# Convolution after attention, one core: q's first block by three queues, band 8 of the second convolution by the two-row way, paired outer products copied by one instruction

## The chip, the cores and the metric

The kernel runs on one core of a Trainium2 chip. The metric is the device time of one execution in microseconds, given as the median of several runs. A profile of one execution lies beside it. The page calls TensorE PE (its weight loads PEld), VectorE DVE, ScalarE ACT, GpSimd POOL and SyncE SP.

## What is computed

The input has 4 images of 128 channels and 64 x 64 pixels, all fp32. Layer 0 is attention, layer 1 a residual block of two 3 x 3 convolutions:

```python
# layer 0
x_norm = _group_norm(x, norm_w, norm_b)                      # 8 groups
qkv = jnp.einsum('oc,bchw->bohw', qkv_w, x_norm) + qkv_b     # 4 heads of 32
attn = jax.nn.softmax(jnp.einsum('bhid,bhjd->bhij', q, k) * scale, axis=-1)
out = jnp.einsum('oc,bchw->bohw', proj_w, attn_times_v) + proj_b
x = x + out
# layer 1
out = conv3x3(x, lsq_quantize(w1, alpha1))                   # 9 taps, pad 1
out = relu(batchnorm(out, gamma1, beta1))                    # mean and variance over all images
out = conv3x3(out, lsq_quantize(w2, alpha2))
out = relu(batchnorm(out, gamma2, beta2) + x)
```

Both batch norms need the mean and the variance over all images before anything after them can start, so each convolution ends in a short serial step.

## The kernel before, in words

**Attention** takes some 2200 us. It goes over 32 blocks (4 images of 8 blocks of 512 query pixels), and in each over 32 steps of 128 key pixels, with two pairs of heads in a step. `scores` (lines 435 to 449) makes the products of one pair (the tiles `s`) and ACT takes their exponential; `weights` (line 461) multiplies by v. `run_scores(3)` and `run_weights(3)` alternate to the end. The order is written out by hand (`manual_schedule`): every engine does its instructions in program order, and waits come from the tiles that they share.

**The first block** is special, because nothing can be hidden ahead of it. `project_parts` makes k, q and v of a chunk of 512 pixels on PE; `parts` (lines 353 to 361) takes a product out of PSUM twice: ACT writes its rounded part and DVE what is left (`kst`, `qst`). For chunk 0 `direct` (lines 396 to 409) then spreads these by eight transfers over the partitions of the tile that the score products read. Their issue alternates between SP and POOL. For q each transfer is 128 KB, and they are written in the order group 0 (four of them), group 1 (four). The first score pair reads group 0 and the second group 1. The later chunks of k go by way of DRAM (`kd`, line 361, stored by SP at this stage, and loaded by `load_k`, line 416). All this is emitted in the order k of chunk 0, q of chunk 0, k 1, v 0, k 2, v 1, k 3, v 2, k 4, v 3.

**A convolution** goes over 16 bands of 16 rows (4 images of 4 bands). fp32 rows are split into a rounded part (hi) and a remainder (lo), and PE does both. There are two ways:

- A *plain* band has 2 tiles of 18 matmuls each, 36 in all. Preparing it (`split_parts`) is one ACT copy for hi (line 619) and one DVE subtraction for lo (line 622). Its statistics are taken by two `bn_stats` on DVE (line 955), and ACT copies the two tiles to `cv` (line 961).
- A *mixed* band makes two output rows at a time out of four products over mixed input rows, with 24 matmuls (`conv_by_two`, line 870). `mixed_parts` prepares it: DVE makes `vo` and the two halves of `vi` (lines 600 to 603), ACT copies both as hi (`uo`, `ui`, line 605), and DVE subtracts for lo and li (line 609). `rows_of_two` (lines 874 to 904) puts the rows together. `copy`: ACT copies the second inner product into the odd rows of `cv`. `inner`: DVE makes even and odd rows from it and the first inner product, with their sums (lines 887 and 889). `outer`: ACT copies the two outer products to `co` with their sums (line 894), and a POOL transfer adds `co` to `cv` in place (line 896). For bands 13 and 14 `outer_at_once` does that addition on DVE instead (line 900). Later ACT squares the band for the variance (line 1011); that is kept in a list (`behind`) and done about two bands later by `flush(1)`, because it must wait for the transfer.

`BY_TWO` (line 584) says which bands are mixed: 2 to 14 in the first convolution, 2 to 14 without 8 in the second. (Band 1 of the first has plain products and its sums from ACT, lines 964 and 968.) `banks` (line 978) gives a band its PSUM: the inner products take two adjoining banks from the pool `pss` (3 tiles of two banks). The outer products take, in turns, another `pss` tile (names ending in z) or two single banks from `psa` (x and y).

`layer` (lines 932 to 1049) is the loop over bands. In band m it emits PE's matmuls of band m, then `copy`, in the first convolution a `flush(1)`, then `begin` (the mixing for band m + 2 with ACT's hi copies), `flush(1)`, `inner`, `rest` (lo and li of band m + 2), `later` (in the first convolution the load of band m + 3, in the second ACT's normalisation of band m + 3, line 1138), and `outer`. After band 14 come the squares that are left, sums on DVE (lines 1027 to 1035), band 15 as two tiles `c_last` with `bn_stats` on DVE (line 1041), and `batch_norm`. Band 15 is prepared in band 13 (`split_parts`).

After the second convolution `load_res` (line 1175) has brought the residual back, and the output goes out chunk by chunk (lines 1201 to 1203).

Of the kernel before, what the change touches and what calls it, by code (L numbers as in the profile page):

```python
# [16 lines left out]
F32 = mybir.dt.float32  # L17
AF = mybir.ActivationFunctionType
ALU = mybir.AluOpType
# [3 lines left out]
P = 128  # L23
# [4 lines left out]
FB = 512  # L28
# [50 lines left out]
def _fast_body(ctx, tc, x, norm_w, norm_b, qkv_wt, qkv_b, proj_wt, proj_b,  # L79
               w1, alpha1, gamma1, beta1, w2, alpha2, gamma2, beta2, out, cnt):  # L80
    nc = tc.nc
    B, C, H, W = x.shape
# [131 lines left out]
    pss = ctx.enter_context(tc.tile_pool(name="pss", bufs=3, space=PSUM))  # L214
# [11 lines left out]
    sums = att.enter_context(tc.tile_pool(name="sums", bufs=2))  # L226
# [5 lines left out]
    def f32(t):  # L232
        return t.bitcast(F32)
# [154 lines left out]
    def k_tile(b, j):  # L388
        ks[b, j] = stack_tile(f"k{b}_{j}")[:, : 2 * FB].rearrange("p (g n) -> p g n", n=FB)
        return ks[b, j]  # L390
# [5 lines left out]
    def direct(what, t):  # L396

        u = k_tile(0, 0) if what == "k" else q_tile(0, 0)
        engines = nc.sync, nc.gpsimd
        for g in range(2):  # L400
            for c, s in enumerate((0, 2, 1, 3)):
                i, part = divmod(s, 2)
                h = 2 * g + i
                src = t[h * D : (h + 1) * D, :, :]
                eng = engines[(4 * g + c) % len(engines)]
                if what == "k":
                    eng.dma_start(out=f32(u)[s * D : (s + 1) * D, g, :], in_=src[:, part, :])
                else:
                    eng.dma_start(out=f32(u)[s * D : (s + 1) * D, g, :, :], in_=src)
# [152 lines left out]
    def raw_band(i, b, g):  # L562
        mixed = b * (H // BR) + g in BY_TWO[i]
        t = stack_tile(f"t{i}_{b}_{g}")
# [13 lines left out]
    raw, ready = {}, {}  # L578
# [2 lines left out]

    BY_TWO = set(range(2, 15)), set(range(2, 15)) - {8}

    def mixed_parts(t, name):

# [45 lines left out]
    def parts_of(i, m, t):  # L633
        b, g = bandlist[m]
        way = mixed_parts if m in BY_TWO[i] else split_parts
        mix, rest, ready[i, b, g] = way(t, f"{i}_{b}_{g}")
        return mix, rest
# [225 lines left out]
    def conv_by_two(parts, a, c, i):  # L863

        for m, ps, w in ((1, a[0], wmix[:, 0, :, :]), (2, a[1], wmix[:, 1, :, :]),
                         (0, c[0], wq[i][:, 0:3, :]), (3, c[1], wmix[:, 2, :, :])):
            n = 0
            for part in parts:
                for kw in range(3):
                    nc.tensor.matmul(ps.rearrange("p (r w) -> p r w", w=W), w[:, kw, :],  # L870
                                     part[m][:, :, kw : kw + W], start=(n == 0), stop=(n == 5))
                    n += 1

    def rows_of_two(a, c, y, sums, name, at_once):

        def of(t, e):
            return t.rearrange("p (r e w) -> p r e w", e=2, w=W)[:, :, e, :]

        even, odd = of(y, 0), of(y, 1)
        a0, a1, c0, c1 = (u.rearrange("p (r w) -> p r w", w=W) for u in (*a, *c))  # L880
        outer_rows = f32(stack_tile(f"co{name}"))[:, : 2 * FB]

        def copy():
            nc.scalar.copy(odd, a1)

        def inner():
            nc.vector.scalar_tensor_tensor(even, odd, 1.0, a0, ALU.mult, ALU.add,
                                           accum_out=sums[:, 0:1])
            nc.vector.scalar_tensor_tensor(odd, odd, -1.0, a0, ALU.mult, ALU.add,
                                           accum_out=sums[:, 1:2])  # L890

        def outer():
            for e, u in enumerate((c0, c1)):
                nc.scalar.activation(of(outer_rows, e), u, AF.Identity,
                                     accum_out=sums[:, 2 + e : 3 + e])
            nc.gpsimd.dma_start(out=y, in_=outer_rows, accum_op=ALU.add)

        def outer_at_once():
            for e, u, v in ((0, even, c0), (1, odd, c1)):
                nc.vector.scalar_tensor_tensor(u, u, 1.0, v, ALU.mult, ALU.add,  # L900
                                               accum_out=sums[:, e : e + 1])

        return copy, inner, outer_at_once if at_once else outer, outer_rows
# [26 lines left out]
    def layer(i, prepare, start=None):  # L930


        on_act = {1} if i == 0 else set()
        plain = [m for m in range(len(bandlist) - 1) if m not in BY_TWO[i] and m not in on_act]
        two = [m for m in range(len(bandlist) - 1) if m in BY_TWO[i] or m in on_act]
        st = mid.tile([P, 2 * len(plain), 6], F32, name=f"st{i}")
        sums = mid.tile([P, 4 * len(two)], F32, name=f"sums{i}")
# [39 lines left out]
        def banks(m):  # L977
            b, g = bandlist[m]
            a = conv_tile(i, b, g)
            if (len(two) - 1 - two.index(m)) % 2:  # L980
                c = [psa.tile([P, FB], F32, name=f"c{i}_{b}_{g}{j}", tag="a") for j in "xy"]
            else:
                c = pss.tile([P, 2, FB], F32, name=f"c{i}_{b}_{g}z", tag="s")
                c = [c[:, j, :] for j in range(2)]
            return [a[:, j, :] for j in range(2)], c

        done = start(banks, stats, keep, origin) if start else {}
        for m, (b, g) in enumerate(bandlist[:-1]):
            if m in done and m not in BY_TWO[i]:
                continue  # L990
            begin, rest, later = prepare(m)
            if m in BY_TWO[i]:
                if m in done:
                    a, c = done[m]
                else:
                    a, c = banks(m)
                    conv_by_two(ready[i, b, g], a, c, i)
                y = cv[b][:, 2 * g * FB : (2 * g + 2) * FB]
                k = two.index(m)
                copy, inner, outer, junk = rows_of_two(a, c, y, sums[:, 4 * k : 4 * k + 4], f"{i}_{m}",  # L1000
                                                       m > 12)
                copy()
                if i == 0:
                    flush(1)
                begin()
                flush(1)
                inner()
                rest()
                later()
                outer()  # L1010
                behind.append(lambda y=y, k=k, junk=junk: nc.scalar.activation(  # L1011
                    junk, y, AF.Square, bias=shift[:, 1:2], accum_out=squares[:, k : k + 1]))
                continue
            ps = conv_tile(i, b, g)
            for j in range(2):
                conv(ready[i, b, g], ps[:, j, :], j, wq[i])
            begin()
            flush(1)
            rest()
            later()  # L1020
            for j in range(2):
                stats(m, j, ps)
                keep(m, j, ps)
            if m == 0:
                origin()
# [10 lines left out]
        b, g = bandlist[-1]  # L1036
        for j in range(2):
            ps = psa.tile([P, FB], F32, name=f"c{i}_last{j}", tag="a")
            conv(ready[i, b, g], ps, j, wq[i])
            c = 2 * g + j  # L1040
# [53 lines left out]
    def opening(banks, stats, keep, origin):  # L1094
        last = parts[len(blocks) - 1]
        last["merge"]()
        e = [conv_tile(0, *bandlist[m]) for m in range(2)]
        conv(ready[0, 0, 0], e[0][:, 0, :], 0, wq[0])
        begin, rest = parts_of(0, 2, raw[bandlist[2]])
        begin()  # L1100
        load_band(*bandlist[3])
        conv(ready[0, 0, 0], e[0][:, 1, :], 1, wq[0])
        mix_weights(0)
        rest()
        last["residual"]()
        for j in range(2):
            stats(0, j, e[0])
            keep(0, j, e[0])
        origin()
        conv(ready[0, 0, 1], e[1][:, 0, :], 0, wq[0])  # L1110
        last["sums"](0)
        last["sums"](1)
        last["spread"]()
        begin, rest = parts_of(0, 3, raw[bandlist[3]])
        begin()
        load_band(*bandlist[4])
        conv(ready[0, 0, 1], e[1][:, 1, :], 1, wq[0])
        rest()
        last["invert"]()
        last["gather"]()  # L1120
        for j in range(2):
            stats(1, j, e[1])
            keep(1, j, e[1])
        done = banks(2)
        conv_by_two(ready[0, 0, 2], *done, 0)
        begin, rest = parts_of(0, 4, raw[bandlist[4]])
        begin()
        rest()
        load_band(*bandlist[5])
        return {0: None, 1: None, 2: done}  # L1130

    a1, c1 = layer(0, first, opening)
# [14 lines left out]
    for r0, r1 in ((0, RB + 2), (RB + 2, BR + 2)):  # L1147
        a, e = max(r0 + g0 * BR - 1, lo_row), min(r1 + g0 * BR - 1, hi_row)
# [45 lines left out]
    for b in range(B):  # L1194
        for j in range(4):
            ends = (b, j) in ((0, 0), (B - 1, 3))
            for p in range(2 if ends else 1):
                n = HN // 2 if ends else HN
                y = res[b, j][:, p * n : (p + 1) * n]
# [463 lines left out]
```

## Time and profile before

| what | us |
|---|---|
| median of 3 runs (2469.05 to 2471.85) | 2470.35 |
| the profiled execution itself | 2469.57 |
| its span, first to last instruction | 2467.9 |
| attention, to PE's last `acc` product | 2226.7 |
| first convolution, to PE's last `c_last` product | 2226.7 to 2330.4 |
| second convolution, to PE's last `c_last` product | 2334.0 to 2437.3 |
| last statistics and output | 2437.3 to 2467.9 |

| engine | busy us | share of the span |
|---|---|---|
| PE | 2432.5 | 99% |
| DVE | 2197.6 | 89% |
| ACT | 2182.4 | 88% |
| POOL | 300.3 | 12% |

The time outside the span (2469.57 less 2467.9) is 1.7 us. The ends of matmuls are modelled and consecutive matmuls overlap, so the spacing of PE's starts is used for what PE needs, and not the mean duration of one matmul. In a row of the timeline the first number is the start in us from the span's beginning, the second the duration; what stands in brackets is the idle time of the engine before it, and what ended it.

### The profile page before, as it was taken

The numbers are of one execution on the slowest core, as the hardware profiler recorded it, in microseconds if no ns is written. First come the engines' busy times: TensorE is split into PE (matmuls) and PEld (weight loads), VectorE is DVE, ScalarE is ACT, GpSimd is POOL, SyncE is SP. The second block draws the span as 40 slices with busy tenths as digits, with TensorE's granted clock in tenths as the row PEclk, the third lists the DMA queues.
The fourth block names the chain that finished last, engine by engine and source line by source line (L and its number), as shares of the span: only waits on it lengthen the run. The fifth ranks groups of instructions, "written<-read, shape, count | busy, mean of one in ns | idle before, by whom it ended". The sixth has DMA issues, their size and how long they took to land.

```text
span 2467.9 us, 65119 instructions
## 1 busy us (share of the span) xinstructions
PE 2432.5 (99%) x28396; PEld 1445.7 (59%) x28396; DVE 2197.6 (89%) x1560; ACT 2182.4 (88%) x2446; POOL 300.3 (12%) x527
## 2 busy tenths in 40 slices
PE   9999999999999999999999999999999999999995
PEld 6555555555555555555555555555555555557774
DVE  6899888989998888899989888898999999999897
ACT  5999888999988899999998899999999999996686
POOL 1111111111101111111101111111010100111110
PEclk9999999999999999999999999999999999999997
DMA  6887677678776766688767676678666666766627
GB/s 195 191 191 167 172 176 176 167 187 210 169 164 167 181 161 163 145 205 205 172 151 175 173 175 156 156 190 204 149 141 147 149 138 144 160 150 167 162 56 236
DMA packets 128389, 416.21 MB, mean 169 GB/s; under 512 B 33808, under 2 KB 34960, under 8 KB 99424
## 3 DMA queue, kind: packets, MB, share of 16 engines
q0 software_dynamic: 48688, 292.38, 52.3%
q1 hardware_dynamic: 78832, 118.54, 17.1%
q8 instruction: 225, 3.69, 0.6%
q10 hardware_dynamic: 576, 1.05, 0.1%
q14 instruction: 68, 0.56, 0.1%
HBM read 107.75 MB, written 56.43 MB: 67 GB/s over the span
## 4 chain that ended last, share of the span: by engine, by line
PE 93%; DVE 3%; DMA 2%; issue 1%; ACT 0%; SPq 0%; POOL 0%; POOLq 0%; ACTq 0%; DVEq 0%
PE s L447 43%; PE acc L461 39%; PE c L837 2%; PE c L870 1%; DMA rm<-p 1%; PE pk L322 1%; PE l L493 1%; PE pq L322 1%; PE pv L322 1%; PE po L322 1%; PE c_last L837 1%; DVE res L1201 1%; DVE li L609 0%; DVE lo L609 0%; DMA cv<-co 0%
## 5 line engine op out<-in xcount | busy, mean ns | idle before, releaser
L449 ACT ACTIVATE p<-s 128x1024 f32<-128x1024 f32 x2048 | 1951.3, 1033 | 197.3 <-PE s L447 153.1
L476 DVE TENSOR_TENSOR r<-r,p 128x2048 f32<-128x2048 f32 x768 | 1757.9, 2289 | 63.1 <-ACT p L449 12.0
L447 PE MATMUL s<-q,k 64*128 64x512 f32 x8192 | 1137.3, 409 | 1.9 <-issue 1.7
L461 PE MATMUL acc<-p,v 128*32 128x256 f32 x16384 | 1025.8, 383 | 0.0
L447 PEld LDWEIGHTS s<-q,k 64*128 64x128 f32 x8192 | 716.1, 184 | 408.3 <-issue 166.2
L461 PEld LDWEIGHTS acc<-p,v 128*32 128x32 f32 x16384 | 462.7, 109 | 483.1 <-issue 248.1
L471 POOL DMA_DIRECT2D rm<-p x160 | 140.4, 877 | 780.3 <-ACT p L449 658.2
L357 DVE SCALAR_TENSOR_TENSOR kst<-pk,b,kst 128x512 fp32r<-128x512 f32 x32 | 24.0, 751 | 80.5 <-PE s L447 61.7
L474 DVE TENSOR_TENSOR r<-p,p 128x2048 f32<-128x2048 f32 x32 | 73.2, 2287 | 8.3 <-ACT p L449 7.0
L357 DVE SCALAR_TENSOR_TENSOR qst<-pq,b,qst 128x512 fp32r<-128x512 f32 x32 | 24.0, 750 | 59.2 <-PE s L447 46.5
L361 POOL DMA_DIRECT2D qd<-qst x31 | 23.0, 742 | 267.1 <-DVE qst L357 217.7
L497 POOL DMA_DIRECT2D r<-rm x32 | 27.2, 851 | 224.6 <-PE s L447 81.2
L870 PE MATMUL c<-ui,wmix 128*128 128x512 f32 x150 | 43.9, 400 | 0.0
L870 PE MATMUL c<-li,wmix 128*128 128x512 f32 x150 | 43.8, 400 | 0.0
L361 POOL DMA_DIRECT2D kd<-kst x27 | 20.0, 741 | 177.3 <-DVE kst L357 162.1
L605 ACT CAST uo<-vo 128x1024 fp32r<-128x1024 f32 x25 | 26.3, 1054 | 16.0 <-DVE vo L600 15.0
L469 POOL DMA_DIRECT2D rm<-p x32 | 17.8, 558 | 175.2 <-ACT p L449 106.9
L1011 ACT ACTIVATE co<-cv,shift 128x1024 f32<-128x1024 f32 x25 | 28.8, 1152 | 11.1 <-DMA cv<-co 11.1
L493 PE MATMUL l<-r,ones 128*32 128x256 f32 x512 | 37.7, 379 | 0.0
L538 POOL DMA_DIRECT2D y<-x x32 | 21.0, 657 | 121.6 <-DVE x L537 112.8
L356 ACT ACTIVATE kst<-pk,b 128x512 fp32r<-128x512 f32 x32 | 22.4, 700 | 14.5 <-PE pk L322 14.5
L322 PE MATMUL po<-av,wp 128*32 128x512 f32 x256 | 33.4, 593 | 0.4 <-DVE av L527 0.4
(268 smaller groups left out, 1220.2 us busy)
## 6 DMA issues: line engine op xcount, KB each, us to landing
rm<-p POOLq DMA_DIRECT2D x192, 1024.0 KB, 7.7
r<-rm POOLq DMA_DIRECT2D x32, 1024.0 KB, 7.6
q<-qd SPq DMA_DIRECT2D x248, 128.0 KB, 4.5
x<-in_x_dram SPq DMA_DIRECT2D x86, 256.0 KB, 6.2
k<-kd SPq DMA_DIRECT2D x124, 128.0 KB, 4.8
qd<-qst POOLq DMA_DIRECT2D x31, 512.0 KB, 5.0
kd<-kst POOLq DMA_DIRECT2D x27, 512.0 KB, 4.4
cv<-co POOLq DMA_DIRECT2D x21, 512.0 KB, 4.8
```

Of the source, the lines that this page charges most:

```text
L322: nc.tensor.matmul(out[cs, :], w[:, cs], x, start=True, stop=True)
L357: nc.vector.scalar_tensor_tensor(lo, ps[what], bias, t[:, 0, :], ALU.add, ALU.subtract)
L361: (nc.sync if start else nc.gpsimd).dma_start(out=dst[b, j].rearrange("s p n -> p s n"), in_=t)
L447: nc.tensor.matmul(s[:, i, :], k[r, half, c0 : c0 + P], q[r, half, part, :], start=(part == 0), stop=(part == 1))
L449: nc.scalar.activation(pts[step][:, 2 * half : 2 * half + 2, :], s, AF.Exp, scale=SCALE)
L461: nc.tensor.matmul(acc[n][h * D : (h + 1) * D, cs], v[:, kt % KB, h * D : (h + 1) * D], pt[:, h, cs], start=(kt == 0 and half == 0), stop= ...
L471: nc.gpsimd.dma_start(out=msum[n], in_=pt, accum_op=ALU.add)
L474: nc.vector.tensor_tensor(rsum[n], pts[step - 1], pt, ALU.add)
L476: nc.vector.tensor_tensor(rsum[n], rsum[n], pt, ALU.add)
L493: nc.tensor.matmul(t["l"][h * D : (h + 1) * D, cs], ones, r[:, h, cs], start=first, stop=end)
L837: nc.tensor.matmul(ps.rearrange("p (r w) -> p r w", w=W), w[:, tap, :], part[:, r0 + kh : r0 + kh + RB, kw : kw + W], start=(n == 0), stop ...
L870: nc.tensor.matmul(ps.rearrange("p (r w) -> p r w", w=W), w[:, kw, :], part[m][:, :, kw : kw + W], start=(n == 0), stop=(n == 5))
```

## The change

Five edits:

1. `direct`: for q the four-fold cycle is SP, POOL, ACT, POOL; so SP issues two of q's eight transfers, ACT two and POOL four. k stays with SP and POOL.
2. `BY_TWO`: band 8 of the second convolution is mixed too.
3. `rows_of_two`: `copy` writes into the first half of the tile `co` instead of the odd rows of `cv`, and `inner` reads it there. `outer` overwrites that tile.
4. `outer`: where the outer products lie in one `pss` tile, one ACT instruction copies both and takes one sum.
5. `layer`: in the first convolution the `flush(1)` ahead of `begin` is left out for bands 13 and 14.

Since the second convolution then has 13 mixed bands instead of 12, and `banks` counts from the last, bands 2, 4 and 6 change places with 3, 5 and 7 as to the pool of their outer products. Bands 9 to 14 keep theirs.

```diff
-        engines = nc.sync, nc.gpsimd
+        engines = (nc.sync, nc.gpsimd) if what == "k" else (nc.sync, nc.gpsimd, nc.scalar, nc.gpsimd)
...
-    BY_TWO = set(range(2, 15)), set(range(2, 15)) - {8}
+    BY_TWO = (set(range(2, 15)),) * 2
...
-    def rows_of_two(a, c, y, sums, name, at_once):
+    def rows_of_two(a, c, both, y, sums, name, at_once):
...
+        copied = outer_rows[:, :FB].rearrange("p (r w) -> p r w", w=W)
+
         def copy():
-            nc.scalar.copy(odd, a1)
+            nc.scalar.copy(copied, a1)
 
         def inner():
-            nc.vector.scalar_tensor_tensor(even, odd, 1.0, a0, ALU.mult, ALU.add,
+            nc.vector.scalar_tensor_tensor(even, copied, 1.0, a0, ALU.mult, ALU.add,
                                            accum_out=sums[:, 0:1])
-            nc.vector.scalar_tensor_tensor(odd, odd, -1.0, a0, ALU.mult, ALU.add,
+            nc.vector.scalar_tensor_tensor(odd, copied, -1.0, a0, ALU.mult, ALU.add,
                                            accum_out=sums[:, 1:2])
 
         def outer():
-            for e, u in enumerate((c0, c1)):
-                nc.scalar.activation(of(outer_rows, e), u, AF.Identity,
-                                     accum_out=sums[:, 2 + e : 3 + e])
+            if both is not None:
+                nc.scalar.activation(
+                    outer_rows.rearrange("p (r e w) -> p e r w", e=2, w=W),
+                    both.rearrange("p e (r w) -> p e r w", w=W), AF.Identity,
+                    accum_out=sums[:, 2:3])
+            else:
+                for e, u in enumerate((c0, c1)):
+                    nc.scalar.activation(of(outer_rows, e), u, AF.Identity,
+                                         accum_out=sums[:, 2 + e : 3 + e])
             nc.gpsimd.dma_start(out=y, in_=outer_rows, accum_op=ALU.add)
...
                 c = [psa.tile([P, FB], F32, name=f"c{i}_{b}_{g}{j}", tag="a") for j in "xy"]
+                both = None
             else:
-                c = pss.tile([P, 2, FB], F32, name=f"c{i}_{b}_{g}z", tag="s")
-                c = [c[:, j, :] for j in range(2)]
-            return [a[:, j, :] for j in range(2)], c
+                both = pss.tile([P, 2, FB], F32, name=f"c{i}_{b}_{g}z", tag="s")
+                c = [both[:, j, :] for j in range(2)]
+            return [a[:, j, :] for j in range(2)], c, both
...
                 copy()
-                if i == 0:
+                if i == 0 and m < 13:
                     flush(1)
                 begin()
```

The rest of the diff passes `both` on.

More of the change, by code (lines that the diff above doesn't have):

```diff
@@ L993, in layer @@
                 if m in done:
-                    a, c = done[m]
+                    a, c, both = done[m]
                 else:
-                    a, c = banks(m)
+                    a, c, both = banks(m)
                     conv_by_two(ready[i, b, g], a, c, i)
@@ L999, in layer @@
                 k = two.index(m)
-                copy, inner, outer, junk = rows_of_two(a, c, y, sums[:, 4 * k : 4 * k + 4], f"{i}_{m}",
+                copy, inner, outer, junk = rows_of_two(a, c, both, y, sums[:, 4 * k : 4 * k + 4], f"{i}_{m}",
                                                        m > 12)
                 copy()
-                if i == 0:
+                if i == 0 and m < 13:
                     flush(1)
@@ L1124, in opening @@
         done = banks(2)
-        conv_by_two(ready[0, 0, 2], *done, 0)
+        conv_by_two(ready[0, 0, 2], *done[:2], 0)
         begin, rest = parts_of(0, 4, raw[bandlist[4]])
```

## The prediction

> **What bounds the kernel now.** I read the page's parts 1 and 4 first, then the chain of waits at the start and in the convolutions, then the timelines of single engines there. PE bounds all of it:
>
> ```profile
> PE 2432.5 (99%) x28396; PEld 1445.7 (59%) x28396; DVE 2197.6 (89%) x1560; ACT 2182.4 (88%) x2446; POOL 300.3 (12%) x527
> PE 93%; DVE 3%; DMA 2%; issue 1%; ACT 0%; SPq 0%; POOL 0%; POOLq 0%; ACTq 0%; DVEq 0%
> ```
>
> From 24.84 to 2437.3 us PE has hardly a gap (the longest, between the convolutions, is 1.3 us). So a gain ahead of the attention, or PE time saved in a convolution, reaches the end, as long as no other engine takes over. Three places matter. The first is the start of the attention, in the chain of waits:
>
> ```profile
> 22.24 0.87 PE pv L322 x32
> 23.11 1.72 issue
> 24.84 3.28 PE s L447 x12
> 28.12 2.29 PE pv L322 x64
> 30.41 1.59 PE s L447 x9
> ```
>
> PE waits 1.72 us for q, and then does its first twelve score products in 3.28 us where later ones take 1.60. Two things are in that: a second wait (0.38 us, to 25.72) ahead of the second pair, and the clock, which the stretches from 25.6 to 28.5 us show at 0.50. The issues of q are
>
> ```profile
> 18.23 3.40 SPq L409 DMA_DIRECT2D q<-qst  x4
> 21.72 1.84 SPq L361 DMA_DIRECT2D kd<-kst  x1
> 18.09 1.94 POOL L409 DMA_DIRECT2D q<-qst  x4
> ```
>
> The second place is the end of the first convolution:
>
> ```profile
> 2313.64 0.58 ACT L884 COPY cv<-c 128x512 f32<-128x512 f32 x1
> 2317.01 1.15 ACT L1011 ACTIVATE co<-cv,shift 128x1024 f32<-128x1024 f32 x1 [2.78 <-DMA cv<-co]
> 2318.16 1.17 ACT L619 CAST hi<-t 128x1188 fp32r<-128x1188 f32 x1
> 2319.36 1.40 DVE L622 TENSOR_TENSOR lo<-t,hi 128x1188 fp32r<-128x1188 f32 x1 [2.91 <-ACT hi L619]
> 2321.51 2.39 PE L837 MATMUL c_last<-hi,wq 128*128 128x512 f32 x9 [0.65 <-DVE cv L900]
> ```
>
> ACT waits for a transfer to square band 11; behind it stands band 15's hi copy, then DVE's lo and band 13's outer rows, whose PSUM `c_last` needs. PE could have gone on at 2320.7. The third is the second convolution:
>
> ```profile
> 2385.77 8.57 PE c L837 x36
> 2428.70 8.62 PE c_last L837 x36
> 2430.82 1.15 ACT L1011 ACTIVATE co<-cv,shift 128x1024 f32<-128x1024 f32 x1 [3.15 <-DMA cv<-co]
> 2434.36 0.17 DVE L1030 TENSOR_REDUCE end<-squares 128x1 f32<-128x12 f32 x1 [3.49 <-ACT co L1011]
> 2437.34 0.70 DVE L1041 BATCH_NORM_STATS2 end<-c_last 128x6 f32<-128x512 f32 x1 [1.56 <-PE c_last L837]
> ```
>
> Band 8 costs PE 8.57 us. At the end DVE waits 3.49 us for the squares, which waited for band 12's transfer, and then only 1.56 us for PE: the squares are the next bound, 1.6 us behind PE.
>
> **What the Trainium skill says.** "DMA: Bandwidth & Descriptors", *Issuing engines are not separate DMA queues*: transfers issued by several engines run on the same 16 DMA engines, and only the issue time is saved. The trace agrees: SP's four issues end at 21.6 us, but the semaphore counts of q's transfers are full at 21.8, 24.75, 25.40 and 25.56 (SP's four) and 21.6, 23.8, 24.6 and 24.9 (POOL's). So the DMA engines limit them, not the queue; they are busy 0.8 to 1.0 from 18.5 us on. "TensorE: Matmul & The Clock Gate", *What's actually happening*: the clock falls to half after an idle window of about 3.4 us, free-running. Here it was half for 3.41 us from 25.51; the window before held some 1.85 us of idle PE (54%). Between the convolutions 1.3 us idle in a window (38%) cost nothing. "ScalarE: Activation LUTs", *What ACT_TABLE_LOAD costs*: 186 ns and 0.833 ns for each element, 93 of them overlapped. By that estimate one copy of 1024 takes 0.95 us, two of 512 take 1.04.
>
> **q by three queues.** POOL keeps its four issues at the same times. SP issues its two by 19.4 instead of 21.6; ACT its two at about 17.2 to 18.3 (two at 0.47 to 0.59 us each, from `x` on ACT and `q` on SP), after it has waited for DVE's part of `qst` (17.15). That wait and issue stand ahead of the next `kst` on ACT (17.10, so 1.1 to 1.2 us later); DVE's lo and the v evacuation follow, and PE's third pv may start 0.3 us late, which the idle PE from 23.11 hides (0.3 if it did not). SP's `kd` store of 512 KB moves from 21.72 to about 19.9, and there it competes with q. In the trace q's last transfer was full at 25.56, when nearly all of the `kd` bytes had moved too; the same 1.8 MB in the same stretch now end at about the same time, with the `kd` part earlier. So the first pair (group 0) gains some 0.5 us, the second, which decides, between -1.1 (all of q behind `kd`, whose count was full at 26.81) and +0.8 (POOL's last, 24.9). **I take 0.3 us**, and the clock still falls.
>
> **The flush in bands 13 and 14 of the first convolution.** The hi copy runs right after the copy at 2313.64, so at 2314.1, hi is ready at 2315.3; DVE finishes `inner` at 2316.4, then lo to 2317.8 and band 13's rows to 2319. PE goes on at 2320.7 instead of 2321.51: 0.8, less a little: **0.7 us**. The wait for the transfer stays on ACT, but behind it are only band 14's copy and squares, and those had 3.2 us to spare (DVE's sums ended at 2327.2, PE's second tile at 2330.4). Bound: 0 to 0.8.
>
> **`copied` and the new wait.** `outer` on ACT now waits until `inner` has read the tile. In the first convolution ACT started `outer` at 2294.05 and `inner` ended at 2294.34, so some 0.3 us a band. Queued behind it on ACT are the next copy and square; POOL's transfer and the PSUM of the outer products wait for it. ACT idled 0.86 us a band ahead of `uo` (2297.79 and others), which hides it: 0; without that cover 10 bands by 0.3, 3 us. In the second, the normalisation (1.2 to 1.3) and the square (1.14) lie between, and `inner` is over 2 us before: 0.
>
> **Paired outer products.** Six bands in each convolution. ACT's spacing is 0.57 us for a 512 copy with its sum, so 1.14; for 1024 from PSUM the exponential's spacing is 0.95, with the sum's 0.10: 1.05. Gain 0.09 a band on ACT, from -0.3 (the strided write slower) to +0.2. ACT is not last in either convolution: 0.
>
> **Band 8 mixed.** PE: a mixed band takes 5.73 us (2.85 + 2.87 in the chain), so 8.57 - 5.73 = 2.84 less. ACT: hi copies 1.95 for 1.08, copy, outer and square 2.66 for 0.96, so +2.6. DVE: vo, vi, vi, lo, li are 1.14 + 0.60 + 0.60 + 1.13 + 1.14 = 4.61 for 1.31, +3.3; `inner` 1.33 for two statistics of 0.65. POOL: four memsets and a DMA issue of 0.87; it is idle. DVE's 3.3 find room: it waited 1.51, 0.73 and 0.96 us around band 8. But then it has no room left: its spacing in mixed bands is 5.94 to 6.01 (lo at 2365.29, 2371.23, 2377.24), over PE's 5.73. li of band 7 ended at 2379.59, and PE needed it at 2380.60 (fourth matmul); 1.0 us of lead at 0.24 a band is gone by band 11, and then **DVE sets the pace**. li of band 14: 2378.37 + 7 x 5.96 + 1.22 = 2421.3, where it was 2421.4. Band 14 starts 0.72 before that, 2420.6 instead of 2422.81. So `c_last` starts 2.2 us earlier, and its second tile ends at 2435.1 instead of 2437.3. Then the squares: ACT's schedule is no earlier, so the square of band 12 is still at about 2430.8, DVE's sums end at 2435.1 as before, the first `bn_stats` (0.69) comes after them, and the second starts at 2435.8 instead of 2437.34: 1.5. The loads of the residual for image 2 wait for PE and now come 2 us sooner, so band 12's transfer (8.1 us to land among them) may land earlier; the most is PE's 2.2. **I take 1.7 us** (bounds 1.0 to 2.2).
>
> **Sum.** 0.3 + 0.7 + 1.7 = 2.7. The profiled execution took 2469.57 (span 2467.9 and 1.7 around it), so 2466.9; it lies 0.8 under the median of 2470.35, so the median goes to 2467.6.
>
> **Rivals.**
> 1. *The clock stays up.* If q lands 0.5 us sooner and PE idles under some 1.3 us, the half clock for 3.41 us (1.7 us of work) goes too. For it: the window held 54%, and 38% was harmless. Against: the DMA engines are full. The window is free-running, so executions may differ. 2.7 + 0.5 + 1.7 = 4.9: 2465.4.
> 2. *q lands later*, behind `kd`: -1.1 instead of +0.3: 2469.0.
> 3. *The slower one: the last accumulating transfer.* In the second convolution band 12's transfer stands among the residual's loads, which now start sooner. The loads land some 1.5 us apart; with three more ahead of it, it takes 12.6 us instead of 8.1, the squares and the second `bn_stats` come 4.5 later than 2435.8, that is 2.9 after the old 2437.34, and with 1.0 gained before: 2472.2. It decides against the change from a landing of 10.7 us. Against it: the loads that wait for PE leave the queue sooner as well.
>
> **How the numbers follow.** Forecast 0.54 (2467.6), the clock 0.22, q later 0.15, the transfer 0.09. The range reaches from the clock's case with the upper bounds, 2464.8, to 2471.3, under the last one. A measurement of this kernel tells 0.2% (4.9 us, below 2465.4 or above 2475.3) from no change. Faster by that: most of the upper half of the clock's case with some of the other bounds, 0.17; slower: the tail of the last, 0.05; the same 0.78.
>
> **What would show it.** Right: the first scores at about 24.3 with the second pair at about 25.4; the clock at half for one window; no idle PE ahead of the first convolution's `c_last`; PE with small waits for li from band 11 of the second convolution on, where DVE idles nowhere; the second `bn_stats` right behind the first. Wrong: the score products at full clock, ACT waiting for `inner` ahead of `uo`, or band 12's transfer taking over 10 us.

## The result, and the profile after

| kernel | median us | lowest to highest | runs |
|---|---|---|---|
| before | 2470.32 | 2468.42 to 2471.85 | 14 |
| after | 2465.21 | 2464.05 to 2466.57 | 14 |

The ratio is 0.9977, with a 95% interval of 0.9970 to 0.9984: 5.1 us faster, 0.21% (interval 4.0 to 7.4 us). The forecast was 2467.6, 2.7 us faster. The time lies in the range that was given (2464.8 to 2471.3), but the gain is nearly twice the forecast, and past the 0.2% to which the prediction gave 0.17. The profiled execution of after took 2465.8 us (span 2464.1), 3.8 us less than that of before.

Parts 1 and 4 of the page of after, first lines: PE bounds more of the chain than before (96% for 93%).

```profile
PE 2430.9 (99%) x28384; PEld 1443.6 (59%) x28384; DVE 2199.4 (89%) x1566; ACT 2183.7 (89%) x2428; POOL 301.8 (12%) x530
PE 96%; DMA 1%; DVE 1%; issue 0%; ACT 0%; SPq 0%; ACTq 0%; POOLq 0%; DVEq 0%; POOL 0%
```

**Start of the attention.** The chain of waits of after from 18.9 us on (start, length, what). The first product of the projections starts 0.74 us later in this execution than in the one of before (14.42 and 13.68), so 0.74 has to be taken off each start when the two are laid side by side.

```profile
18.94 5.57 DMA q<-qst
24.51 0.04 issue
24.56 1.13 PE s L447 x4
25.68 0.10 issue
25.78 1.40 PE s L447 x8
27.18 1.89 PE pv L322 x64
29.06 1.60 PE s L447 x12
```

The 64 products of `pv` took 2.29 us in the profile of before and take 1.89 here; the twelve scores are down from 3.28 to 2.62 (24.56 to 27.18), with the wait for the second pair in them. There is no stretch at half clock (a granted clock of 0.50) at the start of the attention in this trace.

**End of the first convolution.** Timelines of ACT, DVE and PE of after:

```profile
2312.24 1.20 ACT L619 CAST hi<-t 128x1188 fp32r<-128x1188 f32 x1
2316.61 1.15 ACT L1020 ACTIVATE co<-cv,shift 128x1024 f32<-128x1024 f32 x1 [3.17 <-DMA cv<-co]
2314.05 1.39 DVE L622 TENSOR_TENSOR lo<-t,hi 128x1188 fp32r<-128x1188 f32 x1
2319.92 2.31 PE L837 MATMUL c_last<-hi,wq 128*128 128x512 f32 x9
```

ACT still waits 3.17 us for the transfer, but the hi copy now runs 4.4 us ahead of that square, and `c_last` shows no idle time ahead of it.

**End of the second convolution.** The chain and DVE's timeline of after:

```profile
2424.89 8.60 PE c_last L837 x36
2430.63 0.17 DVE L1039 TENSOR_REDUCE end<-squares 128x1 f32<-128x13 f32 x1 [2.94 <-ACT co L1020]
2433.52 0.70 DVE L1050 BATCH_NORM_STATS2 end<-c_last 128x6 f32<-128x512 f32 x1 [1.47 <-PE c_last L837]
```

The squares are in at 2430.63, and DVE then still waits 1.47 us for PE: the end is PE's, not the squares'.

The table gives three stages for every profiled execution of this study, in us: from the first product of the projections to the seventh pair of scores ("start"), and from a convolution's first product to the start of its last `bn_stats`. A star marks executions whose trace has a stretch at half clock at the start of the attention. The medians stand beside the median of the kernel before in the same session.

| kernel | start | conv 1 | conv 2 | median (before) |
|---|---|---|---|---|
| before | 20.54* | 103.76 | 103.35 | |
| after | 18.47 | 102.96 | 101.19 | 2465.21 (2470.32) |
| e1, q alone | 18.44 | 104.57 | 103.36 | 2468.57 (2470.34) |
| e2, all but q | 19.06 | 102.95 | 101.14 | 2466.41 (2470.34) |
| e3, long filler on before | 19.60 | 104.29 | 103.36 | 2469.55 (2470.34) |
| e4, flush alone | 19.27 | 103.31 | 103.34 | 2469.14 (2470.34) |
| e3b, short filler on before | 19.07 | 103.87 | 103.35 | 2468.57 (2469.83) |
| e5, band 8 alone | 20.54* | 104.39 | 101.47 | 2468.67 (2469.83) |
| e7, q two and six | 21.01* | 103.88 | 103.35 | 2469.32 (2469.83) |
| e8, v chunk first on after | 17.78 | 102.96 | 101.16 | 2464.46 (2469.83) |
| e6, band 8 and `copied` | 20.64* | 103.99 | 101.31 | one run |
| e11, band 8 and paired | 21.09* | 104.07 | 101.49 | one run |
| e9, e8 and square later | 17.56 | 102.96 | 100.50 | 2464.03 (2470.20) |
| e10, e9 and chunk between | 17.99 | 102.96 | 101.18 | 2464.13 (2470.20) |

From the seventh pair to the end of the attention the stretch takes 2191.8 to 2193.0 us in these executions, with no order by edit; so a stage above is read to 0.1 us, and a whole execution is not. The ratios of the edits taken singly (e1, e4, e5) all have 1.0 in their intervals. What an edit is worth is therefore read from the stages, each of them in one execution of a kernel.

### The profile page after: what moved, and what is told of

It reads as the page before. It is cut to its first block, busy times and chain, and to the rows that moved or that the text cites. A ratio compares the mean times of both kernels' runs of the same rounds, so it can differ in the third digit from the quotient of the medians.

```text
span 2464.1 us, 65084 instructions
## 1 busy us (share of the span) xinstructions
PE 2430.9 (99%) x28384; PEld 1443.6 (59%) x28384; DVE 2199.4 (89%) x1566; ACT 2183.7 (89%) x2428; POOL 301.8 (12%) x530
## 4 chain that ended last, share of the span: by engine, by line
PE 96%; DMA 1%; DVE 1%; issue 0%; ACT 0%; SPq 0%; ACTq 0%; POOLq 0%; DVEq 0%; POOL 0%
PE s L447 44%; PE acc L461 39%; PE c L870 3%; PE c L837 1%; PE l L493 1%; PE po L322 1%; PE pq L322 1%; PE pv L322 1%; PE pk L322 1%; PE c_2z L870 1%; DMA rm<-p 1%; PE c_0z L870 1%; PE c_last L837 1%; DVE res L1210 1%; PE c_1x L870 0%; PE c_3x L870 0%
## 5 line engine op out<-in xcount | busy, mean ns | idle before, releaser
L904 POOL DMA_DIRECT2D cv<-co x22 | 19.0, 865 | 126.8 <-ACT co L902 41.6
```

## The experiments

**First theory and rivals.** Theory A: the part that was missed is q's, with the landing (0.5 to 0.7 us) and the half clock (1.7 us). Theory B: only the landing. Theory C: it was all in the convolutions.

**e1: edit 1 alone.**

```diff
-        engines = nc.sync, nc.gpsimd
+        engines = (nc.sync, nc.gpsimd) if what == "k" else (nc.sync, nc.gpsimd, nc.scalar, nc.gpsimd)
```

> The kernel before with edit 1 alone: q's eight transfers by SP, POOL, ACT, POOL; both convolutions as before. Theory A (q lands sooner, PE idles less ahead of the first scores, and so the half clock for 3.4 us goes too): about 0.5 us for the landing and 1.7 for the clock, 2.1 us under the kernel before, and no stretch at half clock between 20 and 32 us; the first twelve score products take about 2.5 us instead of 3.3. Theory B (the forecast: only the landing changes): 0.3 to 0.7 us under it, and a stretch of 3.4 us at half clock stays. Theory C (the convolutions made all of the gain): no difference.

Measured: 2468.57 (2467.59 to 2471.52, 13 runs), 1.8 us under before by the medians; the ratio 0.9996 (0.9988 to 1.0005) by itself cannot be told from no change. Its trace tells more. It begins at the same moment as that of before (18.05 and 18.09 for POOL's first issue of q), so starts can be compared directly:

```profile
18.17 5.66 DMA q<-qst
23.84 0.04 issue
23.88 2.49 PE s L447 x12
26.37 1.88 PE pv L322 x64
28.25 1.60 PE s L447 x12
```

The first score is at 23.88 where it was at 24.84: 0.96 sooner. The semaphore count of q's last transfer is full at 24.91 (25.56), and `kd`'s at 26.20 (26.81), so `kd`, though issued 1.7 us sooner, took nothing from q: all of it ended 0.6 us sooner. There is no half clock in the trace. Theory C falls. By this trace A holds; whether the half clock hangs on q alone is for the next runs.

**e2: all but edit 1** (after, with the line above undone).

> The kernel after with edit 1 undone: q's transfers by SP and POOL as before, all edits of the convolutions kept. Theory A: 3.0 us under the kernel before (0.8 in the first convolution, 2.15 in the second), so 2.1 over the kernel after, and the half clock for 3.4 us is back at about 25.5 us. Theory B: 4.4 to 4.8 under the kernel before. Theory C: 5.1 under it, as the kernel after.

Measured: 2466.41, 3.9 us under before, ratio 0.9985 (0.9978 to 0.9991). The convolutions are as short as in after (table), which is 3.0 us of it against the profile of before, and 3.4 against the mean of like executions (see e4). Theory A said that the half clock is back at 25.5 us. It is not in this trace, though q goes as before and PE waits 1.09 and 0.49 us. So the half clock is no fixed part of the kernel before. The windows of the clock say why. In the traces the granted clock changes only at multiples of 3.41 us from where it first rises: before it rises at 5.03 us, falls at 25.51 (20.48 later, six times 3.41) and rises at 28.93; in e7 the stretches are 6.83, 3.41, 13.65 and 3.41 long. So windows of 3.41 us are counted here from the first rise in each execution (7.49 in e2). A row has the stretch and its length, the busy time of PE, PEld, DVE, ACT and POOL with counts, the granted clock, the DMA share and GB/s. Before, where the second window is at half clock:

```profile
22.10:25.51 3.41, 1.69 (x40) 1.22 (x32) 1.89 (x3) 0.69 (x1) 0.00 (x0) 1.00 0.91 288
25.51:28.93 3.42, 3.42 (x31) 2.45 (x32) 0.00 (x0) 2.65 (x3) 0.00 (x0) 0.50 0.33 99
```

e2, where the same waits fall into two windows, and neither is followed by half clock:

```profile
21.14:24.56 3.42, 2.70 (x84) 2.09 (x76) 2.64 (x5) 1.38 (x2) 0.75 (x2) 1.00 0.88 239
24.56:27.97 3.41, 2.56 (x24) 1.68 (x28) 0.55 (x1) 1.68 (x2) 0.00 (x0) 1.00 0.48 173
```

The windows begin at another phase in each execution. With PE busy 1.69 us of 3.41 the clock fell, with 2.56 it did not. **New theory, A2:** with q as before, the half clock comes in some executions only, by the phase; a shorter wait ends it. The mean granted clock of every run, printed to three places, carries it: the traces with 0.994 (before, e5, e7) all have such a stretch. It undercounts, since e6 and e11 have the stretch at a printed 0.995. (e7 has a second one, from 12.47 to 15.88 us, ahead of the projections.) In the first session 22 of 49 runs of before had 0.994 or less, median 2471.2, and 27 had 0.995, median 2469.13: 2.1 us apart (1.9 and 1.3 in the other two sessions), and 3.41 us at half clock are 1.7 us of work. Of all runs of before in these sessions 53 of 110 had the lower clock; of the runs with q by three queues (after, e1, e8, e9, e10) 2 of 61, both in e1.

**e3: a filler on PE ahead of the scores.**

```diff
             load_k(0, j + 1)
+    keep_warm(12)
```

> The kernel before with twelve small products of a constant (128x128 each, about 0.12 us, 1.4 us in all) put on PE between the last product of the first v chunks and the first score product; q's transfers as before, nothing else changed. It takes the idle time of PE away without making q land sooner. Theory A: the clock stays full, the first twelve scores take about 2.5 us, and the time is 1.7 us under the kernel before though the first score starts no sooner. Rival: the slow scores are no matter of PE's idle time (the half clock comes in any case, or the products wait for data): no difference, half clock for 3.4 us stays.

Measured: 2469.55, ratio 0.9997 (0.9988 to 1.0005). The filler was mis-sized: each product is two instructions on PE, so it took 2.9 us and held the first score back to 26.54. Still, all of its 13 runs had a clock of 0.995, and the next twelve scores began sooner than before (30.01 against 30.33). So filling the idle time keeps the clock up; the price was not measured here. So once more, shorter:

**e3b: the short filler** (`keep_warm(6)` at the same place).

> The kernel before with six calls of the small product (twelve instructions, 1.45 us of PE work) between the last product of the first v chunks and the first score product, which fits in the 1.72 us that PE waits for q there; no transfer is changed. Theory: the half clock after the wait comes in some executions only, by where PE's idle time falls against a window of 3.4 us, so these products end it: no run with the lower mean clock, and the time is that of those runs of the kernel before whose clock stayed up, 2469.1 us, 1.2 under its median. Rival (the idle time has nothing to do with it): as the kernel before, 2470.3 us, with the lower mean clock in four of ten runs.

Measured: 2468.57 against 2469.83 in the same session, 1.26 us (ratio 0.9994, 0.9986 to 1.0002), 12 of 13 runs at 0.995 with a median of 2468.51; the runs of before with that clock had 2468.84 and the others 2470.7. No run at the lower clock was expected, and one came. So A2 holds in direction and size, though the ratio alone does not settle it. The chain of e3b:

```profile
22.99 1.53 PE idle L315 x12
24.53 0.18 issue
24.71 2.21 PE s L447 x12
26.91 1.88 PE pv L322 x64
```

**e4: edit 5 alone** (`if i == 0 and m < 13:` ahead of the first `flush(1)`).

> The kernel before with edit 5 alone: the square ahead of the hi copy left out in bands 13 and 14 of the first convolution, so it comes behind it. Theory: PE's gap ahead of c_last (0.65 us in the chain, some 0.8 with the small waits) goes: 0.7 to 0.8 us under the kernel before. Rival: the squares behind it, or band 14's copy, come late and the gap turns into a wait of DVE's sums ahead of the batch norm: 0 to 0.3.

Measured: 2469.14, 1.2 us under before (ratio 0.9996, 0.9987 to 1.0004). By the trace `c_last` starts 94.20 us after the convolution's first product. In six executions with the square ahead of the hi copy (before, e1, e3, e3b, e5, e7) it was 94.89 to 95.69, mean 95.26, so 1.06 is won there. The rival shows as well: the squares came late in this execution, both `bn_stats` followed them back to back (1.29 us in one row), and the convolution ended at 103.31, 0.8 under the mean of those six (104.13).

```profile
2327.51 0.17 DVE L1030 TENSOR_REDUCE end<-squares 128x1 f32<-128x14 f32 x1 [5.84 <-ACT co L1011]
2328.23 1.29 DVE L1041 BATCH_NORM_STATS2 end<-c_last 128x6 f32<-128x512 f32 x2
```

The six differ because PE's gap ahead of `c_last` hangs on the landing of a transfer: 0.65 us in the execution of before, 0.76, 0.78, 1.12, 1.13 and 1.15 in the others. In e1 the gap and what ended it read

```profile
2320.30 1.91 PE L837 MATMUL c_last<-hi,wq 128*128 128x512 f32 x7 [1.14 <-DVE cv L900]
2315.81 1.15 ACT L1011 ACTIVATE co<-cv,shift 128x1024 f32<-128x1024 f32 x1 [2.92 <-DMA cv<-co]
```

All five executions with edits 3 to 5 have 102.95 or 102.96. Edit 5 alone was profiled once; whether its late squares are the draw of a landing or go away with edits 3 and 4 is open.

**e5: edit 2 alone** (`BY_TWO = (set(range(2, 15)),) * 2`).

> The kernel before with edit 2 alone: band 8 of the second convolution mixed too, everything else as before. Theory: PE's 2.84 us for band 8 are taken, up to 2.2 of them reach the end because DVE and ACT in a ring set the pace from band 11 or 12 on; with the copy into odd rows kept, DVE's pace is 0.1 us a band slower than in the kernel after, so the gain is 1.5 to 2.2 us on the time and on the span of the second convolution. Rival: the other two edits of the mixed bands (the copy into its own tile, the paired outer products) are what made room for band 8 on DVE and ACT: then well under 1.5 us here, with waits of PE for li of 0.3 us and more a band.

Measured: the second convolution takes 101.47 us in place of 103.35: 1.88 less. The time is 2468.67, 1.2 under before, ratio 0.9994 (0.9986 to 1.0002); 8 of its 13 runs had the lower clock, and the 5 others a median of 2467.12, 1.7 under the like runs of before. The rival (well under 1.5 without the other edits) falls by the stage and by the runs of like clock.

**e6 and e11: band 8 with edit 3, and band 8 with edit 4**, both on the kernel before. e6 has the `copied` tile with the outer products copied one by one; e11 has the paired copy with `copy` writing into the odd rows.

> The kernel before with edits 2 and 3: band 8 mixed and the copy in its own tile; outer products copied one by one. Read by the lengths of the convolutions in the profile (start of the first product to the last bn_stats: the second took 103.35 us before, 101.47 with band 8 alone, 101.19 with all edits). Theory: edit 3 lets DVE's second operation of inner start 0.605 us after the first, where it waited for its store before (0.72), so DVE's pace in the first convolution goes from 5.95 to 5.83 us a band, and the second convolution takes 101.2 to 101.3 us. Rival: the paired outer products made the 0.3 us there, and this stays at 101.45.

> The kernel before with edits 2 and 4: band 8 mixed and the paired outer products; the copy into the odd rows as before. Theory: ACT's 0.14 us in every second band changes nothing: DVE's pace in the first convolution stays 5.95 us a band and the second convolution takes 101.45 us, as with band 8 alone. Rival: 101.2.

Measured: the second convolution takes 101.31 us in e6, 101.49 in e11. DVE's mixed rows start every 5.83 us in the first convolution of e6 (2281.03, 2286.86, 2292.69) and every 5.94 to 5.95 in e11's. The two operations of `inner` in DVE's timeline, first e6, then e11:

```profile
2285.65 0.68 DVE L889 SCALAR_TENSOR_TENSOR cv<-co,c 128x512 f32<-128x512 f32 x1
...
2286.25 0.68 DVE L891 SCALAR_TENSOR_TENSOR cv<-co,c 128x512 f32<-128x512 f32 x1
```

```profile
2288.00 0.68 DVE L887 SCALAR_TENSOR_TENSOR cv<-cv,c 128x512 f32<-128x512 f32 x1
...
2288.72 0.69 DVE L889 SCALAR_TENSOR_TENSOR cv<-cv,c 128x512 f32<-128x512 f32 x1
```

The second operation starts 0.60 us after the first in e6, 0.72 in e11. In e11 it waits for a semaphore that the first counts up when it is through; in e6 it has no wait. So edit 3 gives 0.16 us of the second convolution, and edit 4 none. The last 0.15 (101.31 to 101.16) only comes with both; these runs do not show by what.

**e7: q's transfers two on SP and six on POOL.**

```diff
-        engines = nc.sync, nc.gpsimd
+        engines = (nc.sync, nc.gpsimd) if what == "k" else (nc.sync, nc.gpsimd, nc.gpsimd, nc.gpsimd)
```

> The kernel before with q's eight transfers split two on SP and six on POOL in place of four and four; ACT issues none. Theory A (what helps is that ACT, idle then, issues 0.9 us before SP and POOL are through with k's transfers, so the bytes start sooner): q's first bytes land as before (20.8 us), the last transfer at 25.2 to 25.6, the second pair of scores at most 0.3 us sooner than before. Theory B (what helps is that SP issues fewer: its third issue took 1.55 us[...]): the last transfer lands about 0.65 us sooner (24.9), as with the three queues, and the time is 0.6 us or more under before in runs of the same clock.

Measured: 2469.32 against 2469.83, ratio 0.9997 (0.9989 to 1.0005). Counted from POOL's first issue, the last transfer was full after 8.06 us, where before needs 7.47 and e1 6.86. Theory B falls: taking issues off SP alone, with `kd` moved forward by it just as in e1, makes the last one later. What is left is ACT: its first issue is at 17.14 us in e1, while SP and POOL are busy with k's transfers up to 18.05, and its first bytes land at 20.00 where q's first landed at 20.79. That this is the sooner start, and not the third queue as such, is argued; no run parts the two.

**e8: more work ahead of the first scores**, on after.

```diff
+    for f in first_chunk(4, "v", True):
+        f()
     run_scores(3)
-    for j in (4, 5):
-        for f in first_chunk(j, "v", True):
-            f()
+    for f in first_chunk(5, "v", True):
+        f()
```

> The kernel after with the projection of v's fifth chunk (32 products, 0.95 us on PE) moved from behind the first three pairs of scores to ahead of them; all else as after. Theory: PE still idles about 1.2 us at the start of the attention (0.37 ahead of the first score, the rest ahead of the second pair), which this work fills while q lands: 0.9 to 1.2 us under the kernel after, no run with the lower clock. Rival: the exponentials of the first pairs then come too late for pairs four to six, whose PSUM waits for them, and PE waits there instead: 0 to 0.3 us under it, or slower.

Measured: 2464.46, ratio to before 0.9977 (0.9968 to 0.9986), the same as that of after. The start stage is 0.66 to 0.69 us shorter than in after and e1 (17.78; 18.47, 18.44), less than the 0.9 to 1.2 expected: the second pair still waits for q's last transfers (0.7 us in the twelve scores' 2.37 us). No run had the lower clock.

**e9 and e10: the square behind the normalisation in the second convolution**, with e8's order; e10 moves v's sixth chunk behind the first pair as well.

```diff
                 begin()
-                flush(1)
+                if i == 0:
+                    flush(1)
                 inner()
                 rest()
                 later()
+                flush(1)
                 outer()
```

> The kernel after with v's fifth chunk ahead of the first scores (as in the run of that alone, 0.7 us by its profile), and in the second convolution with ACT's square moved from ahead of the next band's normalisation to behind it. Theory: DVE waits for ACT there in a ring (its mixed rows, ACT's hi copies, the square, the normalisation, DVE again, 5.99 us a band though DVE's own work is 5.84), and PE waits 0.1 to 0.2 us a band for li in bands 12 to 14: the second convolution takes 100.7 to 100.9 us in place of 101.16, and the time is 1.0 to 1.2 under the kernel after. Rival: the squares and outer products come later, and the end waits for them: 101.2 or more.

> As the run of v's fifth chunk first with the later square, and v's sixth chunk moved too: from behind the first three pairs of scores to between the first pair and the second. Theory: PE still waits 0.7 us for q's last transfers ahead of the second pair (25.1), and this work (0.95 us) fills that: another 0.4 to 0.7 us less from the first product to the thirteenth pair. Rival: then pairs four to six wait for the exponentials of the first, which had the time of that chunk before, and nothing is won (within 0.2 us).

Measured: e9 2464.03 (2462.96 to 2466.97), ratio 0.9978 (0.9969 to 0.9986); e10 2464.13 (2463.34 to 2465.15), ratio 0.9976 (0.9967 to 0.9986). Both medians are about 1.1 us under that of after, from other sessions, and the ratios cannot be told from it: a better version is likely, not shown. In e9's trace the ring is broken: DVE's mixed rows start every 5.82 us in the second convolution, PE has no waits for li, and the stage takes 100.50, 0.66 less. In e10 the rival of e9 came: `c_last` starts as early, but the squares came late. DVE's end, e9 and then e10:

```profile
2428.90 0.17 DVE L1042 TENSOR_REDUCE end<-squares 128x1 f32<-128x13 f32 x1 [4.40 <-ACT co L1023]
2430.57 0.70 DVE L1053 BATCH_NORM_STATS2 end<-c_last 128x6 f32<-128x512 f32 x1 [0.26 <-PE c_last L838]
```

```profile
2430.43 0.17 DVE L1043 TENSOR_REDUCE end<-squares 128x1 f32<-128x13 f32 x1 [4.68 <-ACT co L1024]
2431.16 1.29 DVE L1054 BATCH_NORM_STATS2 end<-c_last 128x6 f32<-128x512 f32 x2
```

With PE 0.66 us sooner the squares are the next bound, and the landing of their transfer decides. The other part of e10 did not pay: the chunk fills the wait of the second pair, and pairs five and six then wait 0.20 and 0.18 us for exponentials; its start stage (17.99; the expectation miscounts the seventh pair as the thirteenth) is no shorter than e8's and e9's.

## Why the prediction was wrong, by its steps

**"and the clock still falls"** is the step that failed. It took the half clock of one profiled execution as a constant of the kernel and asked only whether the change removes it there. The traces show it in four of the six executions with q as before and the wait unfilled (before, e5, e6, e11; not e2, e4), and in none of the seven with q by three queues (after, e1, e8, e9, e10) or with the filler (e3, e3b). Its price in the start stage is 1.5 us (mean 20.70 of the four, 19.17 of the two). By the runs' clocks (about half) and the traces (two in three) that is 0.8 to 1.0 us on average, put at nothing in the forecast: the largest of the four misses below. Rival 1 had the right mechanism and even the reason ("executions may differ"), at 0.22. It had 1.7 for certain where 0.8 to 1.0 on average was to be had; that its 2465.4 is so near the measured 2465.21 is luck, since it took the convolutions too small. (In the window ahead of the half clock the prediction counted 1.85 us of idle PE, 54%; the view has 3.41 less 1.69, so 1.72, 50%.)

**q's landing, 0.3.** Measured 0.7 in the start stage (19.17 to 18.45); the first pair 0.96 sooner, the last transfer 0.65. The prediction let the bytes end "at about the same time" and saw only that `kd` moves forward. "The DMA engines limit them, not the queue" left out when the bytes start: it did not use that ACT, free from 17.15 us on, starts q's bytes some 0.8 us sooner (first landing at 20.00 in e1, 20.79 before). The view with the issues had shown that: SP and POOL begin at 18.1 to 18.2, right behind k's. That this start is the cause is argued (e7).

**The flush, 0.7.** Mechanism right, size off: the gap was read in the execution where it was the smallest of six. Its mean is 0.93, `c_last` starts 1.06 us sooner with edit 5 alone, and the first convolution became 1.17 shorter against their mean (104.13 to 102.96), with edits 3 and 4 in it; in the one execution of edit 5 alone it was 0.8.

**Band 8, 1.7.** Mechanism nearly right, size off: 1.88 alone, 2.17 with the other edits, close to the stated bound of 2.2. That `c_last` starts 2.2 us earlier was right: 94.54 us after the convolution's first product before, 92.40 after. "ACT's schedule is no earlier" was the wrong term: band 12's transfer landed 6.3 us after its issue (8.1 before), the squares were in 2.1 us sooner, counted from the convolution's first product, and PE set the end. This is no chance of one execution: the transfer took 7.5 to 9.7 us in the six executions with band 8 plain, and 6.3 to 6.9 in the six with it mixed and the square unmoved (after, e2, e5, e6, e8, e11). The prediction had named this possibility, and did not count it. The pace is not DVE's own work either (5.84) but the ring over ACT's square and normalisation (5.99 a band in after), as e9 shows, where it is 5.82.

**`copied`, 0, and the paired outer products, 0.** The wait of `outer` for `inner` is there, 0.18 us a band, and hidden, as forecast. That the copy in its own tile takes 0.12 us a band off DVE was not seen; with band 8 mixed it is worth 0.16. The paired copy saves ACT 0.14 where 0.09 was forecast, and is worth nothing alone.

**The sum.** 0.7 + (0.8 to 1.0) + 1.17 + 2.17 = 4.8 to 5.0, measured 5.1. By the medians q is worth 1.8 alone (e1) and 1.2 as what e2 lacks of after, with the stages' 1.5 to 1.7 between them. Each of the four terms was taken too small: the clock by 0.8 to 1.0, the other three by 0.4 to 0.5 each. The correction of the profiled execution to the median ("0.8 under the median") also failed: that execution had the half clock and the shortest gap of six ahead of `c_last`, so it stood for the median neither at the start nor in the first convolution. The third rival (the accumulating transfer) did not come; "q later" is refuted. Of the signs that the prediction named, the first scores came at 23.88 in e1 (24.3 was forecast), the clock was full, and the second `bn_stats` waited 1.47 us for PE instead of following the first; `c_last` without idle time ahead came as forecast.

## What to carry to other kernels

A wait that is about as long as half a clock window cost by chance here: read the clock of every run, not only the trace's, before you count its price as present or absent. Where a gap ends on a DMA's landing, one profiled execution gives one draw of it; ask what an order of instructions free of that landing gives, and count the mean. For the first transfer of a chain, look for the engine that is idle when its data are ready: in e1 ACT started q's bytes 0.8 us sooner, and the last of them landed 0.65 sooner although the DMA engines were 0.95 busy.

## What the hardware showed that was not expected

- The clock fell after windows of 3.41 us in which PE was busy 1.69 us (before), and did not after 2.56 (e2) or 3.04 (after). "TensorE: Matmul & The Clock Gate" in the Trainium skill (*What's actually happening*) speaks of an idle window; here a window half idle was enough. The traces give no sharp limit: the six falls in the first 30 us followed 1.69 to 2.15 us (2.15 in e7), but 2.04 in e4 did not do it, nor did 1.85 (e11) and 1.94 (e10) at the last statistics.
- Of two operations on DVE, the second starts 0.72 us after the first where it reads and writes the rows that the first has read, in the tile that the first writes, and 0.60 where its input lies in another tile. In the first case it has a wait for the first, in the second none (e11, e6).
- SP's third issue of q took 1.55 us in before, where its first two took 0.54 and 0.59; with two issues on SP (e1, after) both took 0.59 to 0.62.
- One ACT copy of 1024 from PSUM with its sum has a spacing of 1.00 us; two of 512 have 1.14 (after, before).
